# A graph network in one kernel: an extra stage in layer 2, other softmax batches, and wide products for two matrix powers

## The chip, the cores and the metric

The kernel runs on one core of a Trainium2 chip. A core has a matrix engine (TensorE, "PE" in the profile), a vector engine (VectorE, "DVE"), a scalar engine (ScalarE, "ACT"), GpSimd ("POOL") and SyncE ("SP"). Each engine works through its own queue in order, and engines wait for each other by semaphores. SP, ACT and POOL also issue DMA transfers. The metric is the device time of one execution in microseconds (us), less is better.

## What is computed

There are 50,000 nodes with 64 features and 25,000 edges sorted by destination. Four layers follow each other, each in the form x = x + layer(relu(layernorm(x))). The change touches the last two.

```python
# layer 2: attention over the edges that end in a node, 4 heads of 16
logits = sum(q[dst] * (k[src] + e_k), -1) * scale + es + clip(log(eg), -10, 10)
attn = softmax of logits over the edges of one dst
agg = segment_sum((v[src] + e_v) * attn, dst) @ Wo + bo        # then scaled and shifted by a task vector
x = layer_norm(h + agg) * g1 + b1
x = layer_norm(x + gelu(x @ W1 + b1) @ W2 + b2) * g2 + b2n

# layer 3: out = expm(-t A) h as a Taylor series, A v = segment_sum(w * v[dst], src)
for 4 substeps:
    for k in 1..20: term = scale * A(term) / k; acc += term
```

Layer 3 is a polynomial in A with known coefficients POLY[k]. Power 1 is A h, power 2 is A(A h), and so on. Only nodes with outgoing edges have a nonzero power, and higher powers reach ever fewer rows.

## The kernel before

The nodes are worked on in NQ = 49 blocks of 1024 (a tile of 128 partitions x 8 x 64). Each block has up to 640 edge slots, 5 tiles of 128. Rows of other nodes are fetched by indirect DMAs that POOL issues (helper `gather`, line 1013), 128 rows each. Sums over edges are products with one-hot matrices in bf16 on PE (`slot_hot`, lines 1945 to 1952, makes the one-hot tile `soh` on DVE). The other factor is an f32 value split into three bf16 parts (`split`, line 1089), so each sum takes three products.

**Two ways of summing.** `to_nodes` (lines 1983 to 1993) loads a 128x128 piece of `soh` as weights and streams 64 columns of values: 45 small products per block, and the result has nodes on partitions. `to_sums` (lines 1964 to 1981) loads 64 columns of values as weights and streams up to 512 columns of `soh`, with blocks 0 to 3 in the upper half of the output's partitions and blocks 4 to 7 in the lower half: 18 products per block, and the result `pa` has features on partitions, 4 groups of 128 nodes along the free axis. Layers 0 and 2 use `to_sums`.

**How stages are run.** `Steps` (line 82) and `pipeline` (line 110) run a list of stages over the blocks. In each step every block in flight does its next stage, the oldest block first, and then a new block begins. After each stage a hook is called. In layer 2 the hook is `lists_pace`, which at a rate of 0.7 per call (1.5 at the end) does one more unit of building the lists that the higher powers need: small DVE and PE instructions, and scatters and gathers on POOL's queue. In power 1 it is `rest`, at 0.34 per call, for what is left of that and for a small dense product chain (`dense`, line 2512). The framework then places the instructions into the queues, with the order of the program as priority, and sets buffers and waits: a tile with `bufs=2` makes the third use wait until the first is read.

**Layer 2** (lines 2285 to 2510) has two such pipelines. `up` has the stages fetch (5 gathers of kvg; loads of qt, keys and typ on SP's queue), hots (one-hot tiles noh and types) and logits (products pv and pe, then lg on DVE at lines 2340 to 2342). Four batches of blocks follow, 13, 12, 12 and 12. When the logits of a batch are done, `softmax` (line 2345) turns them, scans along 640 columns on DVE and turns them back into `att`. `down` works on the batch before, beside the logits of the next. Its twelve stages are fetch2, message, sums (`to_sums` and the eviction of `pa`, line 2406), attend (products with wo into `po`, then z on DVE, line 2414), spread1 (the row variance v), turn (scales z into y on DVE, line 2435, turns y by four PE transposes, line 2438, and evicts them as tr on ACT, line 2440), hidden (products ph with w1m, GELU as hid on ACT), product, spread2, finish (turns back, line 2474; x3 on DVE), spread3 and close (stores h3tab). `sums` and `turn` share one PSUM bank, `pa`; `attend` and `finish` share `po`. At line 2502:

```python
for k, (q0, n) in enumerate(batches):
    while up.done < q0 + n:
        up.step()
        if k:
            down.step(q0)
    softmax(k)
```

So the first batch has only `up` steps (the opening), the next three have an `up` and a `down` step each (mixed), and after the last softmax only `down` steps are left (the end).

**Power 1** (lines 2604 to 2632): fetch gathers 5 x 128 rows of h3tab and loads xs and h; scaled makes `soh` and the weighted, split values; sums does `to_nodes` into the PSUM tile `po`, evicts it as `f` on ACT (line 2624), stores `f` to ftab[0] from ACT's queue and adds it to xs with the coefficient. **Power 2** (lines 2638 to 2671) does the same with 2 gathers of ftab[0] per block, 39 small products (line 2663), `f` (line 2666), the store to ftab[1], and the store of xs to the output. `f` has two buffers. The gathers of a power need the whole table of the power before. **Powers 3 to 8** work on lists, with gathers and adding scatters on POOL (line 2720).

Of the kernel before, what the change touches and what calls it, by code (L numbers as in the profile page):

```python
# [22 lines left out]
F32 = mybir.dt.float32  # L23
F16 = mybir.dt.float16
# [949 lines left out]
def fast(ctx: ExitStack, tc: tile.TileContext, a: dict, out: bass.AP, flag: bass.AP):  # L974
# [956 lines left out]

    def load_keys(pool, q, s):

        s.keys = pool.tile([P, RW], F16, name="keys", bufs=4)
        nc.sync.dma_start(s.keys, ktab[q:q + 1, :].to_broadcast([P, RW]))

    def node_hot(pool, s):
# [296 lines left out]
    with tc.tile_pool(name="l1", bufs=2) as pool, \  # L2234
# [25 lines left out]
        def turn(q, s):  # L2260
            s.tr = turned(pool, ps, s.h2, "pt")
# [23 lines left out]
    with tc.tile_pool(name="l2", bufs=2) as pool, \  # L2285
# [3 lines left out]
        etab, typei, wo, bo, b1m, w1m, gcen, w2m, zb, g2c, b2n, half = (  # L2289
            getattr(cp2, x) for x in "etab typei wo bo b1m w1m gcen w2m zb g2c b2n half".split())  # L2290

        batches = [(0, 13), (13, 12), (25, 12), (37, 12)]
        batch_of = {q: k for k, (q0, n) in enumerate(batches) for q in range(q0, q0 + n)}
        S = {q: State() for q in range(NQ)}
        lgs, atts = {}, {}
# [17 lines left out]
        def logits(q, s):  # L2313
            k = batch_of[q]
            q0, n = batches[k]
            if q == q0:
                lgs[k] = pool.tile([P, 5, 13 * NH], F32, name="lg")
            vv = pool.tile([P, 5, D], F32, name="vv")
            lg = lgs[k][:, :, (q - q0) * NH:(q - q0 + 1) * NH]
            es = pool.tile([P, 5, NH], F32, name="es")  # L2320
            kk = pool.tile([P, 5, D], F32, name="kk")
            for i0, m in ((0, 3), (3, 2)):
                pv = ps.tile([P, 3, KW], F32, name="pv", bufs=2)
                for i in range(m):
                    nc.tensor.matmul(pv[:, i, :], s.types[:, (i0 + i) * P:(i0 + i + 1) * P], etab[:, :KW],
                                     start=True, stop=True)
                nc.vector.tensor_add(kk[:, i0:i0 + m, :], s.kv[:, i0:i0 + m, 0:D], pv[:, :m, 0:D])
                nc.vector.tensor_add(vv[:, i0:i0 + m, :], s.kv[:, i0:i0 + m, D:2 * D], pv[:, :m, D:2 * D])
                nc.vector.tensor_copy(es[:, i0:i0 + m, :], pv[:, :m, 2 * D:KW])  # L2329
# [12 lines left out]
            nc.vector.scalar_tensor_tensor(lg, lg, HD ** -0.5, es, op0=OP.mult, op1=OP.add)  # L2342


        def softmax(k):
            q0, n = batches[k]
            R = n * NH
            rep = pool.tile([NQ, 13, NH], F32, name="rep", bufs=1)
            nc.vector.tensor_copy(rep[:, :n, :], ident[:NQ, q0:q0 + n, None].to_broadcast([NQ, n, NH]))
            sm = pool.tile([13 * NH, RW + 1], F32, name="sm", bufs=1)  # L2350
            pen = pool.tile([13 * NH, RW + 1], F32, name="pen", bufs=1)
            rr = rep[:, :n, :].rearrange("q n h -> q (n h)")
            for c0, c1 in ((0, 512), (512, RW + 1)):
                pr = ps.tile([13 * NH, 512], F32, name="pv", bufs=2)
# [3 lines left out]
            row = pool.tile([13 * NH, RW], F32, name="row", bufs=1)  # L2358
            for i0, m in ((0, 4), (4, 1)):
                pt = ps.tile([13 * NH, 4, P], F32, name="pv", bufs=2)  # L2360
# [3 lines left out]
            f = pool.tile([13 * NH, RW], F32, name="fw", bufs=1)  # L2364
            b = pool.tile([13 * NH, RW], F32, name="bw", bufs=1)
# [9 lines left out]
            pt = ps.tile([P, 5, 13 * NH], F32, name="pe")  # L2375
            for i in range(5):
                nc.tensor.transpose(pt[:, i, :R], row[:R, i * P:(i + 1) * P], ident[:R, :R])
            atts[k] = pool.tile([P, 5, 13 * NH], F32, name="att")
            nc.scalar.activation(atts[k][:, :, :R], pt[:, :, :R], AF.Copy)


# [48 lines left out]
        def spread1(q, s):  # L2430
            spread(s, "v1")

        def turn(q, s):
            y = pool.tile([P, 8, D], F32, name="y", bufs=1)
            nc.vector.tensor_mul(y, s.z.rearrange("p i h d -> p (i h) d"), over(invert(s, "r1"), 8))
            pt = ps.tile([P, 4, P], F32, name="pa")
            for i in range(4):
                nc.tensor.transpose(pt[:, i, :], y[:, 2 * i:2 * i + 2, :].rearrange("p a d -> p (a d)"), ident)
            s.tr = pool.tile([P, 512], F32, name="tr")
            nc.scalar.activation(s.tr, pt.rearrange("p i n -> p (i n)"), AF.Copy)  # L2440

# [51 lines left out]
        def close(q, s):  # L2493
# [3 lines left out]

        lists_pace.rate, lists_pace.gap = 0.7, 5
        up = Steps(range(NQ), S, (fetch, hots, logits), lists_pace)
        down = Steps(range(NQ), S, (fetch2, message, sums, attend, spread1, turn, hidden, product, spread2, finish, spread3,  # L2500
                                      close), lists_pace)
        for k, (q0, n) in enumerate(batches):
            while up.done < q0 + n:
# [90 lines left out]
    with tc.tile_pool(name="mps", bufs=1, space=PSUM) as mps, tc.tile_pool(name="l3", bufs=2) as pool, tc.tile_pool(name="pl3", bufs=2, space=PSUM) as ps:  # L2594
# [18 lines left out]
        def scaled(q, s):  # L2613
# [3 lines left out]
                nc.scalar.activation(y3[:, i, 0, :], s.y[:, i, :], AF.Copy, scale=swgt[:, 5 * q + i:5 * q + i + 1])  # L2617
            s.parts = split(y3)

        def sums(q, s):  # L2620
            po = ps.tile([P, 8, D], F32, name="po")
            to_nodes(po, s.soh, s.parts)
            f = pool.tile([P, 8, D], F32, name="f")
            nc.scalar.activation(f, po, AF.Copy)
            nc.scalar.dma_start(nodes(ftab[0], q), f)
            nc.vector.tensor_add(s.xs, s.xs, s.h)
            nc.vector.scalar_tensor_tensor(s.xs, f, float(POLY[1]), s.xs, op0=OP.mult, op1=OP.add)
            if q < NQ - NKEPT:
                nc.sync.dma_start(nodes(xstab, q), s.xs)

        rest = Pace(itertools.chain(lists_pace.work, dense(mp, mps)), 0.34)
        pipeline(range(NQ), (fetch, scaled, sums), rest)
        rest.rest()

        l2 = lists[2]
# [18 lines left out]
            s.parts = split(y3)  # L2654

        def sums2(q, s):
            po = ps.tile([P, 8, D], F32, name="po")
            for j in range(8):
                n = 2 if j >= SECOND else 1
                for o in range(n):  # L2660
                    c = j * P + o * (OW - SECOND * P)
                    for k in range(3):
                        nc.tensor.matmul(po[:, j, :], s.soh[:, c:c + P], s.parts[:, o, k, :],  # L2663
                                         start=(o == 0 and k == 0), stop=(o == n - 1 and k == 2))
            f = pool.tile([P, 8, D], F32, name="f")
            nc.scalar.activation(f, po, AF.Copy)  # L2666
            nc.scalar.dma_start(nodes(ftab[1], q), f)
            nc.vector.scalar_tensor_tensor(s.xs, f, float(POLY[2]), s.xs, op0=OP.mult, op1=OP.add)  # L2668
            store_x(s.xs, q)

        pipeline(range(NQ), (fetch2, scaled2, sums2))


    sums = {}
# [112 lines left out]
```

## Time and profile before

| | us |
|---|---|
| median of 3 runs (lowest, highest) | 3567.95 (3559.2, 3574.22) |
| the profiled execution, whole | 3569.77 |
| its span, first to last instruction | 3568.0 |
| layer 2 in the span | 1730 to 2766 |
| power 1 in the span | 2766 to 3126 |
| power 2 in the span | 3126 to 3280 |
| powers 3 to 8 in the span | 3280 to 3568 |

How to read it: the page gives each engine's busy time and, in 40 slices of 89 us, its busy share in tenths and the clock that was granted to TensorE (5 is half speed). A row of busy times by stretch has the stretch, its length, the busy time and instruction count of PE, weight loads, DVE, ACT and POOL, the granted clock, the busy share of the DMA engines and their GB/s. A row of a wait names who waited and for whom, then the total, the number of times and the longest. A row of a group has the line, engine, operation, tiles, shape and count, then busy time and the mean in ns of one, and then the idle time just before these instructions and what ended it ("issue": nothing that the profile shows). A busy PE isn't a PE at its peak, since matmuls are pipelined. Idle time of an engine that isn't the limit costs nothing.

### The profile page before, as it was taken

What the parts mean: (1) busy time and instruction counts of PE and PEld (TensorE: products, weight loads), DVE (VectorE), ACT (ScalarE), POOL (GpSimd) and SP (SyncE); (2) the same over time, 40 slices, a digit from 0 to 9 for tenths busy, and PEclk for the clock granted to TensorE, in tenths of its full rate; (3) what the DMA queues carried; (4) which work ended last, traced back from release to release, by engine and by line L of the source; (5) the groups of instructions that cost most, each with busy time, mean ns of one, the idle gap of its engine ahead of it and who ended that gap; (6) DMA issues with size and microseconds to landing.
All of it is one profiled execution on the core that took longest, in us unless ns stands there. A gap on an engine that the chain in (4) does not pass through costs nothing. (4 is left out here: it accounts for less than half of the span.)

```text
span 3568.0 us, 62333 instructions
## 1 busy us (share of the span) xinstructions
PE 2492.4 (70%) x21184; PEld 1729.4 (48%) x21184; DVE 2620.7 (73%) x8434; ACT 1328.5 (37%) x2962; POOL 2070.2 (58%) x1955
## 2 busy tenths in 40 slices
PE   7898675399987673477669779889888554356620
PEld 3324565266665452355446445555554443356520
DVE  9999998699998882488677877777878576456410
ACT  0002553144442262377204326646667333333000
POOL 0377777655550477665374127665430787775786
PEclk9755555699996575688657667777779775567555
DMA  1003783487771362478654234343233646377221
GB/s 54 6 4 90 205 234 123 110 224 212 211 200 44 90 197 75 130 234 243 188 145 124 62 90 132 111 122 110 80 94 101 211 139 193 96 216 213 45 26 12
DMA packets 530638, 463.35 MB, mean 130 GB/s; under 512 B 281171, under 2 KB 387954, under 8 KB 530180
## 3 DMA queue, kind: packets, MB, share of 16 engines
q1 hardware_dynamic: 365012, 269.33, 26.5%
q10 hardware_dynamic: 93408, 139.47, 11.3%
q0 software_dynamic: 71888, 50.46, 7.6%
q8 instruction: 169, 2.77, 0.3%
q14 instruction: 161, 1.32, 0.1%
HBM read 226.23 MB, written 233.89 MB: 129 GB/s over the span
## 5 line engine op out<-in xcount | busy, mean ns | idle before, releaser
L1013 POOL DMA_INDIRECT kvg<-kvtab,nrs x245 | 260.6, 1064 | 307.6 <-DVE es L2329 184.0
L1013 POOL DMA_INDIRECT gt<-g1tab,nrs x245 | 243.6, 994 | 238.6 <-DVE lhot L1791 110.6
L1013 POOL DMA_INDIRECT y<-h3tab,sptr x245 | 276.8, 1130 | 138.9 <-issue 68.0
L1013 POOL DMA_INDIRECT ga<-atab,nrs x245 | 250.3, 1022 | 170.4 <-DVE z L2190 60.5
L1991 PEld LDWEIGHTS <-soh 128*128 128x128 bf16 x4410 | 221.7, 117 | 237.0 <-issue 221.8
L1013 POOL DMA_INDIRECT raw<-otab,nrd x196 | 193.4, 987 | 191.9 <-DVE bad L1159 132.5
L1981 PE MATMUL pa<-soh,m 128*64 128x256 bf16 (+3 forms) x1764 | 238.9, 348 | 25.2 <-DVE m L1093 11.6
L1018 POOL DMA_INDIRECT stab<-raw,pf x196 | 207.3, 1058 | 59.8 <-issue 59.8
L1013 POOL DMA_INDIRECT lgot<-nmap,ldst x183 | 190.1, 1039 | 75.3 <-issue 52.8
L1991 PE MATMUL po<-g,soh 128*128 128x64 bf16 x2205 | 123.3, 215 | 145.5 <-DVE g L1093 143.0
L1950 DVE TENSOR_SCALAR soh<-it,key 128x512 bf16<-128x512 f16 (+2 forms) x735 | 210.7, 332 | 1.8 <-PE pa L1981 1.6
L1991 PE MATMUL po<-y,soh 128*128 128x64 bf16 x2205 | 122.3, 228 | 125.9 <-DVE y L1093 65.4
L2272 PE MATMUL pp<-wkv,tr 64*128 64x256 f32 x784 | 151.2, 496 | 52.4 <-ACT tr L2001 52.1
L1013 POOL DMA_INDIRECT y<-ftab,ldst x140 | 138.9, 992 | 75.0 <-issue 45.7
L1093 DVE TENSOR_TENSOR y<-y 128x320 f32<-128x320 f32 (+1 forms) x196 | 75.6, 389 | 140.6 <-ACT y L2617 116.3
L1942 DVE TENSOR_SCALAR noh<-keys,pblk 128x256 bf16<-128x256 f16 (+1 forms) x784 | 176.0, 286 | 2.8 <-DMA keys<-ktab 2.7
L1196 PE MATMUL pab<-wab,tr 64*128 64x128 f32 x784 | 150.3, 437 | 32.5 <-ACT tr L1183 32.5
L1981 PEld LDWEIGHTS <-m 128*64 128x64 bf16 x1764 | 118.0, 119 | 97.9 <-issue 32.5
L1196 PEld LDWEIGHTS pab<-wab,tr 64*128 64x128 f32 x784 | 136.3, 324 | 51.5 <-ACT tr L1183 51.5
L2338 PE MATMUL pe<-qt,noh 128*128 128x64 bf16 x2205 | 157.7, 231 | 0.3 <-DVE noh L1942 0.2
L2720 POOL DMA_INDIRECT out<-y,lnode x85 | 132.4, 1558 | 38.3 <-issue 24.4
L2617 ACT ACTIVATE y<-y,swgt 128x64 f32<-128x64 f32 x245 | 82.2, 345 | 176.6 <-DMA y<-h3tab,sptr 161.1
(607 smaller groups left out, 7496.8 us busy)
## 6 DMA issues: line engine op xcount, KB each, us to landing
kvtab<-kv SPq DMA_DIRECT2D x49, 512.0 KB
ftab<-f ACTq DMA_DIRECT2D x98, 256.0 KB
xt<-in_x SPq DMA_DIRECT2D x96, 256.0 KB
btab<-bt ACTq DMA_DIRECT2D x49, 384.0 KB
bt<-btab SPq DMA_DIRECT2D x49, 384.0 KB
qtab<-qt ACTq DMA_DIRECT2D x49, 384.0 KB
qt<-qtab SPq DMA_DIRECT2D x49, 384.0 KB
xs<-xstab SPq DMA_DIRECT2D x70, 256.0 KB
```

The source lines that it names most:

```text
L1013: return nc.gpsimd.indirect_dma_start(out=dst, out_offset=None, in_=tab[:, :], in_offset=IndirectOffsetOnAxis(ap=idx, axis=0))
L1018: return nc.gpsimd.indirect_dma_start(out=tab[:, :], out_offset=IndirectOffsetOnAxis(ap=idx, axis=0), in_=src, in_offset=None, bounds_chec ...
L1093: nc.vector.tensor_sub(x3[:, :, k, :], x3[:, :, k - 1, :], h[:, :, k - 1, :])
L1196: nc.tensor.matmul(pab[:, i, :], s.tr[r, i, :], wab[r, :], start=True, stop=True)
L1942: nc.vector.tensor_scalar(s.noh[:, j, :n * P], s.keys[:, t0 * P:(t0 + n) * P], pblk[:, j:j + 1], None, op0=OP.is_equal)
L1950: nc.vector.tensor_scalar(oh[:, OHW[i]:OHW[i + 1]], it16[:, b0 * P:(b0 + n) * P], keys[:, q, i:i + 1], None, op0=OP.is_equal)
L1981: nc.tensor.matmul(o, l, r, start=(k == 0), stop=(k == len(t) - 1))
L1991: nc.tensor.matmul(po[:, j, :], oh[:, c:c + P], msg[:, i, k, :], start=(not started and i == t0 and k == 0), stop=(end and (not started or ...
L2272: nc.tensor.matmul(pp[:, i, :], s.tr[r, 2 * k + i, :], wkv[r, :], start=True, stop=True)
L2338: nc.tensor.matmul(pe[:, i, :], s.noh[:, j, c:c + P], s.qt[:, j, k, :], start=False, stop=(j == b0 + nb - 1 and k == 2))
L2617: nc.scalar.activation(y3[:, i, 0, :], s.y[:, i, :], AF.Copy, scale=swgt[:, 5 * q + i:5 * q + i + 1])
L2720: st = nc.gpsimd.indirect_dma_start(out=out[:, :], out_offset=IndirectOffsetOnAxis(ap=s.node[:, t:t + 1], axis=0), in_=sums[k][:, t, :], i ...
```

## The change

1. In layer 2, y = z x 1/std leaves `turn` and becomes a stage `scale1` of its own, ahead of it. `down` has thirteen stages. y gets two buffers instead of one, and the tile keys (used in layers 0 and 2) three instead of four.
2. The batches are 10, 13, 13 and 13 blocks. The widest is still 13, so the softmax tiles keep their shapes.
3. Powers 1 and 2 use wide products: `to_sums` in power 1, and the like of it written out in power 2 (12 products). The result `pa` is evicted as `sums` on ACT, and a fourth stage turns it by four PE transposes into `po`, which is evicted as `f` as before.

```diff
-        s.keys = pool.tile([P, RW], F16, name="keys", bufs=4)
+        s.keys = pool.tile([P, RW], F16, name="keys", bufs=3)
...
-        batches = [(0, 13), (13, 12), (25, 12), (37, 12)]
+        batches = [(0, 10), (10, 13), (23, 13), (36, 13)]
...
+        def scale1(q, s):
+            s.y = pool.tile([P, 8, D], F32, name="y")
+            nc.vector.tensor_mul(s.y, s.z.rearrange("p i h d -> p (i h) d"), over(invert(s, "r1"), 8))
+
         def turn(q, s):
-            y = pool.tile([P, 8, D], F32, name="y", bufs=1)
-            nc.vector.tensor_mul(y, s.z.rearrange("p i h d -> p (i h) d"), over(invert(s, "r1"), 8))
             pt = ps.tile([P, 4, P], F32, name="pa")
             for i in range(4):
-                nc.tensor.transpose(pt[:, i, :], y[:, 2 * i:2 * i + 2, :].rearrange("p a d -> p (a d)"), ident)
+                nc.tensor.transpose(pt[:, i, :], s.y[:, 2 * i:2 * i + 2, :].rearrange("p a d -> p (a d)"), ident)
...
+        def evict(s, pa):
+            s.sums = pool.tile([P, 4, P], F32, name="sums")
+            nc.scalar.activation(s.sums.rearrange("p i n -> p (i n)"), pa, AF.Copy)
+
+        def by_node(s):
+
+            po = ps.tile([P, 4, 2, D], F32, name="po")
+            for i in range(4):
+                nc.tensor.transpose(po[:, i].rearrange("p h d -> p (h d)"), s.sums[:, i, :], ident)
+            f = pool.tile([P, 8, D], F32, name="f")
+            nc.scalar.activation(f.rearrange("p (h i) d -> p i h d", h=2), po, AF.Copy)
+            return f
+
         def sums(q, s):
-            po = ps.tile([P, 8, D], F32, name="po")
-            to_nodes(po, s.soh, s.parts)
-            f = pool.tile([P, 8, D], F32, name="f")
-            nc.scalar.activation(f, po, AF.Copy)
+            pa = ps.tile([P, 512], F32, name="pa")
+            to_sums(pa, s.soh, s.parts)
+            evict(s, pa)
+
+        def store(q, s):
+            f = by_node(s)
             nc.scalar.dma_start(nodes(ftab[0], q), f)
...
-        pipeline(range(NQ), (fetch, scaled, sums), rest)
+        pipeline(range(NQ), (fetch, scaled, sums, store), rest)
...
         def sums2(q, s):
-            po = ps.tile([P, 8, D], F32, name="po")
-            for j in range(8):
-                n = 2 if j >= SECOND else 1
-                for o in range(n):
-                    c = j * P + o * (OW - SECOND * P)
+            pa = ps.tile([P, 512], F32, name="pa")
+            todo = ([], [])
+            for h in range(2):
+                for o, b in ((0, 4 * h), (1, max(SECOND, 4 * h))):
+                    c = b * P + o * (OW - SECOND * P)
+                    n = (4 * h + 4 - b) * P
                     for k in range(3):
-                        nc.tensor.matmul(po[:, j, :], s.soh[:, c:c + P], s.parts[:, o, k, :],
-                                         start=(o == 0 and k == 0), stop=(o == n - 1 and k == 2))
-            f = pool.tile([P, 8, D], F32, name="f")
-            nc.scalar.activation(f, po, AF.Copy)
+                        todo[h].append((pa[h * D:(h + 1) * D, (b - 4 * h) * P:512], s.parts[:, o, k, :],
+                                        s.soh[:, c:c + n]))
+            for k in range(6):
+                for t in todo:
+                    nc.tensor.matmul(*t[k], start=(k == 0), stop=(k == 5))
+            evict(s, pa)
+
+        def store2(q, s):
+            f = by_node(s)
             nc.scalar.dma_start(nodes(ftab[1], q), f)
...
-        pipeline(range(NQ), (fetch2, scaled2, sums2))
+        pipeline(range(NQ), (fetch2, scaled2, sums2, store2))
```

The additions to xs, the loads and the stores that follow each `f` are in `store` and `store2` unchanged.

More of the change, by code (lines that the diff above doesn't have):

```diff
@@ L2290, in fast @@
             getattr(cp2, x) for x in "etab typei wo bo b1m w1m gcen w2m zb g2c b2n half".split())
-        batches = [(0, 13), (13, 12), (25, 12), (37, 12)]
+        batches = [(0, 10), (10, 13), (23, 13), (36, 13)]
+        NB = max(n for _, n in batches)
         batch_of = {q: k for k, (q0, n) in enumerate(batches) for q in range(q0, q0 + n)}
@@ L2316, in logits @@
             if q == q0:
-                lgs[k] = pool.tile([P, 5, 13 * NH], F32, name="lg")
+                lgs[k] = pool.tile([P, 5, NB * NH], F32, name="lg")
             vv = pool.tile([P, 5, D], F32, name="vv")
@@ L2347, in softmax @@
             R = n * NH
-            rep = pool.tile([NQ, 13, NH], F32, name="rep", bufs=1)
+            rep = pool.tile([NQ, NB, NH], F32, name="rep", bufs=1)
             nc.vector.tensor_copy(rep[:, :n, :], ident[:NQ, q0:q0 + n, None].to_broadcast([NQ, n, NH]))
-            sm = pool.tile([13 * NH, RW + 1], F32, name="sm", bufs=1)
-            pen = pool.tile([13 * NH, RW + 1], F32, name="pen", bufs=1)
+            sm = pool.tile([NB * NH, RW + 1], F32, name="sm", bufs=1)
+            pen = pool.tile([NB * NH, RW + 1], F32, name="pen", bufs=1)
             rr = rep[:, :n, :].rearrange("q n h -> q (n h)")
             for c0, c1 in ((0, 512), (512, RW + 1)):
-                pr = ps.tile([13 * NH, 512], F32, name="pv", bufs=2)
+                pr = ps.tile([NB * NH, 512], F32, name="pv", bufs=2)
                 nc.tensor.matmul(pr[:R, :c1 - c0], rr, same[:, c0:c1], start=True, stop=True)
@@ L2357, in softmax @@
             nc.vector.tensor_scalar(pen[:R], sm[:R], -1.0, BIG, op0=OP.add, op1=OP.mult)
-            row = pool.tile([13 * NH, RW], F32, name="row", bufs=1)
+            row = pool.tile([NB * NH, RW], F32, name="row", bufs=1)
             for i0, m in ((0, 4), (4, 1)):
-                pt = ps.tile([13 * NH, 4, P], F32, name="pv", bufs=2)
+                pt = ps.tile([NB * NH, 4, P], F32, name="pv", bufs=2)
                 for i in range(m):
@@ L2363, in softmax @@
                 nc.scalar.activation(row[:R, i0 * P:(i0 + m) * P], pt[:R, :m, :], AF.Copy)
-            f = pool.tile([13 * NH, RW], F32, name="fw", bufs=1)
-            b = pool.tile([13 * NH, RW], F32, name="bw", bufs=1)
+            f = pool.tile([NB * NH, RW], F32, name="fw", bufs=1)
+            b = pool.tile([NB * NH, RW], F32, name="bw", bufs=1)
             nc.vector.tensor_tensor_scan(f[:R], pen[:R, 0:RW], row[:R], -BIG, op0=OP.add, op1=OP.max)
@@ L2374, in softmax @@
             nc.vector.tensor_mul(row[:R], row[:R], b[:R])
-            pt = ps.tile([P, 5, 13 * NH], F32, name="pe")
+            pt = ps.tile([P, 5, NB * NH], F32, name="pe")
             for i in range(5):
                 nc.tensor.transpose(pt[:, i, :R], row[:R, i * P:(i + 1) * P], ident[:R, :R])
-            atts[k] = pool.tile([P, 5, 13 * NH], F32, name="att")
+            atts[k] = pool.tile([P, 5, NB * NH], F32, name="att")
             nc.scalar.activation(atts[k][:, :, :R], pt[:, :, :R], AF.Copy)
@@ L2499, in fast @@
         up = Steps(range(NQ), S, (fetch, hots, logits), lists_pace)
-        down = Steps(range(NQ), S, (fetch2, message, sums, attend, spread1, turn, hidden, product, spread2, finish, spread3,
+        down = Steps(range(NQ), S, (fetch2, message, sums, attend, spread1, scale1, turn, hidden, product, spread2, finish, spread3,
                                       close), lists_pace)
```

## The prediction

> **What bounds the kernel now.** I read the page first, then the busy times by stretch, then the waits of layer 2 and the groups of the two power stretches, and last the timeline.
>
> ```profile
> span 3568.0 us, 62333 instructions
> ...
> PE 2492.4 (70%) x21184; PEld 1729.4 (48%) x21184; DVE 2620.7 (73%) x8434; ACT 1328.5 (37%) x2962; POOL 2070.2 (58%) x1955
> ...
> PEclk9755555699996575688657667777779775567555
> ```
>
> No engine is full over the span, so each stage has a limit of its own. The stretches below are layer 2 (opening, first mixed part, rest of the mixed part, end), power 1 and power 2.
>
> ```profile
> core 0: us, PE busy (x) PEld busy (x) DVE busy (x) ACT busy (x) POOL busy (x), PEclk, DMA share, GB/s
> 1730.00:1852.00 122.00, 73.31 (x842) 54.28 (x841) 82.88 (x341) 6.11 (x12) 86.86 (x82) 0.50 0.58 168
> 1852.00:2125.00 273.00, 222.15 (x1696) 140.15 (x1697) 214.07 (x894) 89.38 (x131) 80.34 (x74) 0.68 0.33 96
> 2125.00:2545.00 420.00, 372.71 (x2467) 229.26 (x2463) 328.12 (x1094) 246.68 (x349) 271.50 (x256) 0.74 0.38 113
> 2545.00:2766.00 221.00, 187.05 (x950) 111.45 (x949) 178.72 (x553) 151.27 (x242) 48.03 (x45) 0.84 0.31 96
> 2766.00:3126.00 360.00, 177.15 (x2365) 151.49 (x2366) 217.06 (x539) 118.21 (x334) 276.82 (x245) 0.63 0.53 159
> 3126.00:3280.00 154.00, 93.63 (x1919) 87.97 (x1918) 92.25 (x244) 57.92 (x147) 99.17 (x98) 0.71 0.87 244
> ```
>
> In the opening POOL sets the pace: the timeline has a kvg gather every 1.25 to 1.4 us, five to a block, and the logits of two blocks 6.7 us apart (lg at 1826.7 and 1833.5). In the mixed part and the end PE is busy 81 to 89% and DVE 78 to 81%; both lose time to each other:
>
> ```profile
> POOL kvg L1013 <- DVE es L2329: 184.0, 15, 33.4
> ACT tr L2440 <- PE pa L2438: 107.0, 35, 6.8
> ...
> DVE z L2414 <- PE po L2412: 88.0, 27, 6.9
> ...
> PE ph L2448 <- ACT hid L2450: 16.5, 20, 2.1
> ...
> PE pa L2438 <- DVE y L2435: 10.3, 9, 2.7
> ```
>
> POOL waits there for buffers that DVE frees, so it isn't the limit. In the powers it is:
>
> ```profile
> L1013 POOL DMA_INDIRECT y<-h3tab,sptr x243 | 274.9, 1131 | 74.1 <-issue 67.7 <-ACT y L2617 3.0 <-DMA y<-h3tab,sptr 2.7
> L1013 POOL DMA_INDIRECT y<-ftab,ldst x98 | 99.2, 1012 | 43.5 <-issue 33.5 <-ACT y L2653 6.7 <-DMA y<-ftab,ldst 2.4
> L2663 PE MATMUL po<-y,soh 128*128 128x64 bf16 x1911 | 92.5, 221 | 57.3 <-ACT f L2666 33.8 <-DVE y L1093 14.8 <-ACT y L2653 6.6
> ...
> L1981 PE MATMUL pa<-soh,m 128*64 128x256 bf16 (+3 forms) x1764 | 238.9, 348 | 25.2 <-DVE m L1093 11.6
> ```
>
> In power 1 (2770 to 3126 here) gathers and their gaps make 274.9 + 74.1 = 349 of 356 us. In power 2 (to 3277) they make 142.7 of 151, and the DMA engines are 87% busy.
>
> **The scaled rows.** No instruction is added: r1 (0.18 us) and y (0.68 us) are issued one step earlier, ahead of the next turn instead of in it. DVE's order inside a step stays (finish, y, reduce, z). PE's transposes of y no longer wait for DVE in the same step: 10.3 us of PE waits go. Behind them ACT waits 107 us for tr, and PE waits 16.5 us for hid, which queues on ACT behind tr; I credit a fifth of that, 3 us. What is late next is z behind the attend products (88 us), PE's own pace, so nothing more is credited. Bounds: -27 (both PE waits go whole) and, since every queue's order can change with a stage more, a loss that rival D prices at 39. Taken: -13, near the row that goes for certain. The second y buffer is paid with one of four keys buffers: in layer 2 typ, with two buffers on the same SP queue, stands behind it and is tighter; in layer 0 keys still come two steps before their use. DVE's wait for keys is 2.7 us in the whole kernel (the page's group of L1942), so 0, and +3 if it doubles. The thirteenth stage makes the drain one step longer, but the same instructions; PE works until 2755 of 2766, so I put 1 us on the last latency.
>
> **The batches.** The opening covers 10 blocks instead of 13: 3 x 6.7 = -20.1 us, of POOL's pace. The three blocks move into mixed steps (39 instead of 36). There each costs PE, from the group rows between 2080 and 2310, 29.6/9.0 + 10.3/9.2 + 8.6/11 = 5.2 us, three 15.6; PE idles 51 of 273 us in the first mixed part, to which they go. Cost between 0 and 15.6; taken 8. The hooks that feed the list building come later with the three blocks: nine hooks x 0.7, six units, +3 (a unit costs DVE and PE a few tenths of a us each: from 0.3-us rows such as lhot's). The end has 13 starts instead of 12, but the pipe behind them is no fuller: 247 stage calls of 13 (19.0 blocks) for 222 of 12 (18.5), which the mixed part is rid of: 0. Softmax instructions run over 640 columns whatever the rows: 0. Sum -9, bounds -20 and -1 (+6 if a unit costs three times that).
>
> **The powers.** Per block 45 (power 1) or 39 (power 2) narrow products become 18 or 12 wide ones, an ACT eviction (0.59 us, 7.1/12 in the rows of L2406) and four f32 transposes. PE before: 92.5/49 = 1.9 us in power 2, 2.5 in power 1. After: the wide products of layers 0 and 2 take 238.9/98 = 2.4 us a block (the halves overlap: 18 x 0.348 would be 6.3), a burst at clock 0.95 took 1.49, the transposes 0.66 at full clock and 1.12 at half. Power 2 has as many columns in its longer half (3 x 1024). So 2.15 us at full clock, some 2.1/c at clock c. In power 1 a block has 7.2 us of POOL: hidden, and POOL's own waits are 6 us: 0. In power 2 a block has 154/49 = 3.1 us: at 0.71, 49 x 2.96 = 145 us and 21 us of waits for y make 166, +12; on the other side, products that no longer wait for f (33.8 us of PE waits) let the stage run closer to POOL, up to -9 (its 6.7 + 2.4 us of waits). Taken: -2, because f's two buffers and their stores (20 us of ACT's waits) stay as they are. ACT goes from 58 to 87 of 154 us. Both stages end with a chain that nothing covers: +0.59 and +1.1 less a shorter burst, +1.5 each. Sum +1, bounds -9 and +64 (next part).
>
> The trace grants 0.71 in power 2 and 0.99 to 1.00 where PE hardly pauses. The Trainium skill (TensorE: Matmul & The Clock Gate, Part 1) says that the clock is halved by default and released by some 3.4 us of steady work: by it a busier PE in power 2 would earn the full clock, 105 us and no cost; by the row 145. Against the change stands TensorEngine Tiling, Key Properties: a change of tiling mode drains TensorE, and each block now changes twice; in layer 2 the wide products followed transposes at 2444.6 without a gap, so I add nothing.
>
> **Sum.** -13 + 1 - 9 + 1 = -20. The profiled execution took 3569.8 us (span 3568.0 and 1.8 around it), 1.8 over the median of 3567.95: 3548.
>
> **Rivals.**
> - A, the forecast, 3548 (3536 to 3560): 0.44.
> - B, the waits change places: z behind PE takes the 13 us, the three blocks cost their full 15.6 + 3. Then 0 + 1 - 1.5 + 1, nothing: 3568. For it: PE is 89% busy from 2125 on. 0.18.
> - E, the queues loosen more: if earlier transposes halve DVE's 88 us for z and that ends last, -44 instead of -13: 3517. For it: a step without list work took 14.0 us (z at 2443.3 and 2457.3) where the mean of 36 is 693/36 = 19.3. Against: most of the rest is list work. 0.16.
> - C, slower: PE becomes the bound of power 2. Its place is the wide products with transposes, its price 49 x 3.95 us (1.49 x 0.95/0.5 + 1.12 at half clock) + 21 = 215 for 154, +61: 3609. It decides from a clock of about 0.77 down (2.1/c + 0.4 over 3.1 us). For it: 0.71 now. Against: more work, fewer pauses. 0.10.
> - D, slower: a new order of instructions in layer 2's queues costs 1 us in each of 39 mixed steps and the y wait returns elsewhere: 3548 + 39 = 3587. For it: steps differ by 5 us already. 0.12.
>
> **Chances.** About 0.5% is what a measurement of this kernel can tell from no change, 3550 and 3586 here. Faster: E and 0.28 of A, 0.44. Within: the other 0.16 of A and 0.14 of B, 0.30. Slower: C, D and the rest of B, 0.26. The range goes from half way beyond E, 3512, to beyond D, 3598.
>
> **What would show it.** Right: no row of PE waiting for y in layer 2; first lg of the second batch some 20 us earlier in the stage; layer 2 some 20 us shorter; power 1 still 349 us of gathers; power 2 within 10 us of 154. Wrong: a longer wait of z or of the first products in place of y's; POOL idle in power 2 with a clock near 0.5; layer 0 longer than 515 us (keys).

## The result and the profile after

The changed kernel takes 3593.61 us (median of 20 runs, 3566.15 to 3617.29). The kernel before, run beside it on the same chip, takes 3568.95 (20 runs, 3559.2 to 3579.44). The ratio is 1.0064, 95% interval 1.0044 to 1.0084: slower by 23 us, 16 to 30. The forecast was 3548, faster by 20. The time lies inside the predicted range, but on the other side of "before".

When e13 to e16 ran, every kernel, the kernel before beside them included, took some 1120 us longer, so of these four only the ratios to that kernel before are used.

The profiled execution after took 3590.18 us, span 3588.4. From its page, the span, the busy times and the granted clock:

```profile
span 3588.4 us, 57871 instructions
...
PE 2580.9 (72%) x18930; PEld 1686.0 (47%) x18930; DVE 2627.9 (73%) x8434; ACT 1353.9 (38%) x3046; POOL 2046.7 (57%) x1955
...
PEclk9755555699996575788567658667788786688555
```

The powers' narrow products are gone (PE has 2254 instructions less), ACT has 84 more, and the clock is higher in the slices of the powers (34 to 37: 6, 6, 8 and 8 tenths, before 5, 5, 6 and 7). Where the time went shows only by stretch. These are layer 2 (opening, mixed part, end), power 1 and power 2 of the kernel after, cut at the eviction of the first and the last `att`, and at the first gather of each power:

```profile
core 0: us, PE busy (x) PEld busy (x) DVE busy (x) ACT busy (x) POOL busy (x), PEclk, DMA share, GB/s
1731.00:1831.00 100.00, 58.47 (x660) 42.81 (x661) 70.39 (x277) 5.96 (x12) 70.47 (x67) 0.50 0.61 172
1831.00:2563.00 732.00, 618.59 (x4327) 380.18 (x4326) 551.65 (x2060) 310.64 (x459) 359.51 (x345) 0.72 0.36 104
2563.00:2801.00 238.00, 198.85 (x963) 117.21 (x961) 182.63 (x547) 157.59 (x248) 47.05 (x45) 0.80 0.31 94
2801.00:3156.00 355.00, 227.80 (x1238) 131.06 (x1238) 218.71 (x537) 140.09 (x383) 267.91 (x246) 0.73 0.55 161
3156.00:3300.00 144.00, 111.77 (x792) 60.78 (x792) 95.33 (x241) 80.71 (x196) 97.58 (x98) 0.94 0.93 257
```

The same cuts in the kernel before are at 1740.4 (first kvg), 1852.1, 2545.7, 2767.5, 3128.7 and 3338.5 (first row of the powers 3 to 8). The lengths, cut alike:

| us | before | after | difference |
|---|---|---|---|
| opening, from the first kvg gather | 111.7 | 91.0 | -20.7 |
| mixed part (36 and 39 steps) | 693.6 | 731.3 | +37.7 |
| end | 221.8 | 238.3 | +16.5 |
| power 1 | 361.2 | 354.9 | -6.3 |
| power 2, to the first row of the list powers | 209.8 | 203.3 | -6.5 |

So layer 2 lost 34 us (opening, mixed part, end) and the powers won 13. The waits of layer 2 after (who waited for whom, total, times, longest), the rows that answer to those of before and the new ones:

```profile
...
ACT L2453 <- PE ph L2451: 104.5, 28, 12.5
DVE z L2415 <- PE po L2413: 81.6, 24, 14.2
ACT v L2472 <- PE pv L2470: 80.2, 18, 25.6
...
ACT tr L2443 <- PE pa L2441: 42.9, 15, 8.6
...
PE pa L1981 <- DVE m L2394: 9.0, 7, 3.8
...
PE ph L2451 <- ACT zt L2463: 7.0, 9, 1.6
...
PE pa L2441 <- DVE y L2436: 4.4, 3, 2.8
```

What the change aimed at happened: PE's wait for y fell from 10.3 to 4.4 us and ACT's for tr from 107.0 to 42.9. In their place ACT waits 104.5 us for the hidden products (24.3 before) and 80.2 for the products pv of spread2 (21.0 before), and PE waits for m and zt, where it hardly did.

### The profile page after: what moved, and what is told of

It reads as the page before. It is cut to its first block, busy times and chain, and to the rows that moved or that the text cites. A ratio compares the mean times of both kernels' runs of the same rounds, so it can differ in the third digit from the quotient of the medians.

```text
span 3588.4 us, 57871 instructions
## 1 busy us (share of the span) xinstructions
PE 2580.9 (72%) x18930; PEld 1686.0 (47%) x18930; DVE 2627.9 (73%) x8434; ACT 1353.9 (38%) x3046; POOL 2046.7 (57%) x1955
## 5 line engine op out<-in xcount | busy, mean ns | idle before, releaser
L1013 POOL DMA_INDIRECT y<-h3tab,sptr x245 | 267.8, 1093 | 171.6 <-DVE soh L1950 97.2
L1981 PE MATMUL pa<-soh,m 128*64 128x512 bf16 (+3 forms) x1764 | 258.3, 364 | 37.1 <-DVE m L1093 15.3
L1981 PE MATMUL pa<-soh,y 128*64 128x256 bf16 (+3 forms) x882 | 138.1, 412 | 87.3 <-DVE soh L1950 61.7
L2451 PE MATMUL ph<-tr,w1m 64*128 64x256 f32 x392 | 144.4, 496 | 24.6 <-ACT hid L2453 16.2
L1991 PEld LDWEIGHTS <-soh 128*128 128x128 bf16 x2205 | 107.9, 114 | 97.9 <-issue 94.6
L1139 ACT ACTIVATE ln_v<-ln_v,epsc 128x8 f32<-128x8 f32 x147 | 43.9, 298 | 276.6 <-DVE ln_v L1138 258.8
L2339 PE MATMUL pe<-qt,noh 128*128 128x64 bf16 x2205 | 141.5, 221 | 0.2
```

What stands on the lines that cost most here:

```text
L1013: return nc.gpsimd.indirect_dma_start(out=dst, out_offset=None, in_=tab[:, :], in_offset=IndirectOffsetOnAxis(ap=idx, axis=0))
L1139: nc.scalar.activation(v, v, AF.Sqrt, bias=epsc, scale=1.0 / D)
L1981: nc.tensor.matmul(o, l, r, start=(k == 0), stop=(k == len(t) - 1))
L1991: nc.tensor.matmul(po[:, j, :], oh[:, c:c + P], msg[:, i, k, :], start=(not started and i == t0 and k == 0), stop=(end and (not started or ...
L2451: nc.tensor.matmul(ph[h][:, c:c + 256], w1m[r, :], s.tr[r, c:c + 256], start=True, stop=True)
```

## The experiments

First theory: the moved y makes every round of layer 2 dearer, because the queues get a new order (rival D's mechanism). Second theory: it is only the depth of the pipeline, and the batches do the rest. In brackets after a ratio stands its 95% interval. The us behind it are that ratio times the median of the kernel before, run beside it, less that median, with the interval's ends.

**The parts alone.** Each is the kernel before with one part of the change's diff. e1 has the scale stage, y's second buffer and three keys buffers. e2 has the batches, e3 the powers. e4 has a stage that does nothing in the new one's place:

```diff
+        def idle(q, s):
+            pass
...
-        down = Steps(range(NQ), S, (fetch2, message, sums, attend, spread1, turn, hidden, ...
+        down = Steps(range(NQ), S, (fetch2, message, sums, attend, spread1, idle, turn, hidden, ...
```

> The kernel before with the scaled rows in a stage of their own and three keys buffers; batches and powers as before. The whole change lost 34 us in layer 2 and won 13 in the powers, so something in layer 2 is dearer. Theory 1 (the move of y itself makes every step of the lower pipeline dearer, as rival D had it: the end part took 237 us for 221, and a mixed step kept its 19 us though it has less list work): +20 to +30 us. Theory 2 (a stage more only costs one more step in which the pipe runs out, 8 us by the last stores of h3tab, which leave every 3.5 to 9 us; the rest of the loss is the batches'): +5 to +10 us. My prediction had -12.

> The kernel before with the batches 10, 13, 13, 13 alone. The opening gets 20.7 us shorter in either theory (att of the first batch came that much earlier in the whole change). Theory 1: the three blocks cost some 27 us in the mixed steps (9.15 us an upper block beside lower work), net +7. Theory 2: they cost more, because in the second batch three of its steps start no lower block (10 blocks are ready for 13 steps), so that the lower pipe has a hole: net +17 to +25. My prediction had -9.

> The kernel before with the wide products and transposes in powers 1 and 2 alone. In the whole change power 1 took 355 us for 361 and power 2 took 141 for 148. Both theories: -13 us, layer 2 unchanged. Rival: part of that gain is an accident of where the stages stood after layer 2, then 0 to -5. My prediction had +1.

> The kernel before with a stage in the place of the new one that does nothing, so that the lower pipeline has thirteen stages and the hook of the list building is called once more per block; y is still made in the turn stage. Theory 1 (it is the move of y): -3 to +4 us. Theory 2 (it is the depth): the same +5 to +10 as with y moved.

Measured: e1 1.0047 [1.0032, 1.0063], +17 (11 to 23). e2 1.0019 [1.0, 1.0037], +7 (0 to 13). e3 0.9957 [0.9939, 0.9975], -15 (-22 to -9). e4 1.0011 [0.9995, 1.0027], +4 (-2 to 10). So the powers win, the batches lose a little, as the first theory had it (+7), and y in a stage of its own loses most. The empty stage's +4 is not clear of zero. Neither theory had e1 right: 17 lies below the first one's 20 and above the second one's 10. In e4 and e1 the end takes 229.3 and 232.3 us for 221.8, which speaks for depth, and in these two profiles the mixed part is as long as before (693.5 and 695.4). So of e1's 17 us some 10 lie in the end by its profile, and next to none in the mixed steps. (Some 8 us of e1's profile lie ahead of layer 2, as 7 of e4's do: the starts of layer 2 in these profiles lie between 1738 and 1749, in code that no experiment touches but for keys.)

**Depth and y apart.** e5 takes a stage away from the kernel before, e8 does the same beside the moved y, so that it has twelve stages again. e7 has both layer 2 edits without the powers.

```diff
             s.parts = split(m3)
+            lists_pace()
+            if q + 1 < NQ:
+                fetch2(q + 1, S[q + 1])
...
-        down = Steps(range(NQ), S, (fetch2, message, sums, ...
+        down = Steps(range(NQ), S, (message, sums, ...
```

> The kernel before with one lower stage less: the loads of fetch2 for the next block are issued at the end of message, in the place in the order where they stood, so that the lower pipeline has eleven stages (the hook is still called twelve times per block); y stays in turn. Theory 2 (depth: each lower stage is one more step at the end, 7.5 us in the profile of the empty stage, 10.5 in that of the scale stage, 221.8 us of end before): -7 to -10 us, all of it in the end part (212 to 215 us). Rival: the longer ends of the two were chance between executions, or came from the hook called more often: 0 (-3 to +3).

> Both layer 2 edits without the powers. The single edits gave +17 and +7 by the times, and the powers -13; together the change gave +23, so 14 us more than the sum. If the two edits really add to each other (the mixed part of the whole change took 731 us for 720 with the batches and 695 with the scale stage alone): +34 to +40. If the sum is the truth and the rest is uncertainty of the intervals (6 us each way): +20 to +28.

> The kernel before with y in a stage of its own (three keys buffers) and fetch2 issued from message, so that the lower pipeline has twelve stages as before. Theory 1 (the move of y itself costs, 13 us by the difference of the scale stage, +17, and the empty one, +4): +8 to +13. Theory 2 (only the depth cost): within 4 us of the kernel before, the end part within 4 us of 222. My prediction's reason (PE no longer waits for y in the same step): -13.

Measured: e5 0.9994 [0.9978, 1.001], -2 (-8 to 4), end 222.3. e8 1.0078 [1.0053, 1.0102], +28 (19 to 36). e7 1.0067 [1.0047, 1.0088], +24 (17 to 31). The second theory, that it is only the depth, falls: a stage less at the front brings nothing, and with the old depth the moved y costs as much as the whole loss, and more than the first theory's 13. In e8 the mixed part takes 725.3 us (690.1 in e5) and the end 220.1: here the loss is in the mixed steps. e7 is the sum of e1 and e2 (17 + 7) by the times.

**The batches the other way.** e6 has batches of 24 and 25, with one buffer each for lg and att.

> The kernel before with two batches, 24 and 25 (lg and att with one buffer each, for room); everything else as before. With the batches 10, 13, 13, 13 the opening got 22.5 us shorter (7.5 a block) and the mixed part 26 longer (8.7 a block). Theory 2a (a block's logits cost more beside lower work, where PE is 86% busy, than in the opening, where POOL sets the pace; lower work costs the same anywhere): 11 blocks moved the other way bring 11 x 1.2 = 13, and two softmaxes go, some 5 to 10 us each: -15 to -33 us. Theory 2b (what cost the time was the hole in the lower pipe, 10 blocks for 13 steps; beside a full pipe the logits are nearly free): opening +82, mixed part shorter by the lower work alone, and the end without logits beside it longer by as much: +30 to +60 us.

Measured: 1.0017 [1.0001, 1.0033], +6 (0 to 12). Both theories miss. The opening took 71 us more, the mixed part 226 less, the end 159 more. How the blocks are divided hardly matters over this span. In e2 the row of the mixed part shows why three blocks more in it cost as much as the opening wins:

```profile
1830.00:2549.00 719.00, 615.85 (x4336) 382.97 (x4336) 553.85 (x2048) 329.02 (x474) 361.19 (x345) 0.71 0.37 107
```

PE is busy 616 us where the kernel before has 595 in its 694, so 21 us more, 7 a block. PE's idle time is 103 us, 99 before. None of the three blocks' work shows up there.

**The order of the queues.** The same products stand in another order on PE when y is ready a step sooner. I take it that the framework puts an instruction ahead when it expects its operands earlier; that is argued from the order and not shown. The timeline of PE shows one round without list work of the kernel before (start, duration, operation; in brackets the idle time before it and what ended it):

```profile
2356.39 0.49 PE L2412 MATMUL po<-wo,sums 128*128 128x128 f32 x2
2356.71 0.60 PE L2438 MATMUL pa<-ident,y 128*128 128x128 f32 x4
...
2358.43 1.86 PE L1981 MATMUL pa<-soh,m 128*64 128x512 bf16 x16
...
2362.47 1.05 PE L2467 MATMUL pv<-half,sqt 128*128 128x2 f32 x8 [0.54 <-DVE es L2329]
...
2365.11 0.34 PE L2325 MATMUL pv<-etab,types 24*128 24x132 bf16 x3
...
2369.09 2.05 PE L2454 MATMUL ph<-tr,gcen 128*128 128x512 f32 x2
```

and the same of e1:

```profile
2369.11 0.60 PE L2440 MATMUL pa<-ident,y 128*128 128x128 f32 x4
...
2373.72 1.39 PE L2469 MATMUL pv<-half,sqt 128*128 128x2 f32 x8 [2.02 <-DVE es L2329]
2374.97 2.05 PE L2456 MATMUL ph<-tr,gcen 128*128 128x512 f32 x2
2376.96 0.51 PE L2325 MATMUL pv<-etab,types 24*128 24x132 bf16 x3
...
2382.41 2.61 PE L1981 MATMUL pa<-soh,m 128*64 128x512 bf16 x7
...
2385.27 1.16 PE L2412 MATMUL po<-wo,sums 128*128 128x128 f32 x8
2386.36 0.74 PE L1981 MATMUL pa<-soh,m 128*64 128x256 bf16 x9
```

Before, the order is attend with the transposes of y, to_sums, pv, logits, gcen. In e1 w1m no longer stands between the transposes of zt and pv, which now waits 2.02 us for DVE's es; gcen stands ahead of the logits, and to_sums is cut in two by attend. Over layer 2, e1's PE waits 10.7 us for m (0.5 before), 11.1 for zt (2.6) and 10.0 for the v of spread2 (1.5). Its waits for y are 9 us less and those for x of finish 10 less. All its waits together are 153 us, 124 before. That sum isn't the cost, though: in e10, which is 22 us faster than e1, PE's waits come to 155 us. The same 630 products of to_sums in the mixed part tell more. In the kernel before, in e1, in e10 and in e17 (the last two hold the old order, see below) their rows are:

```profile
L1981 PE MATMUL pa<-soh,m 128*64 128x512 bf16 (+3 forms) x630 | 76.0, 362 | 5.2 <-ACT tr L2440 4.4 <-DVE m L2393 0.5
L1981 PE MATMUL pa<-soh,m 128*64 128x512 bf16 (+3 forms) x630 | 92.2, 397 | 12.9 <-DVE m L2393 8.7 <-DVE m L1093 2.0 <-ACT tr L2442 1.6
L1981 PE MATMUL pa<-soh,m 128*64 128x256 bf16 (+3 forms) x630 | 65.5, 333 | 14.4 <-ACT tr L2455 13.6 <-DVE m L2395 0.5
L1981 PE MATMUL pa<-soh,m 128*64 128x512 bf16 (+3 forms) x630 | 75.3, 362 | 4.2 <-ACT tr L2444 4.2
```

With y moved and the order free they take 16 us more of PE's time, with y moved and the order held 11 less. The trace's clock records say why: 165 of the 630 ran for the most part at half clock before (154 in e9 and 212 in e3, whose layer 2 has the order of before), 284 in e1, 70 in e10 and 168 in e17. Other products gained in e1 (gcen took 933 ns for 1070), and its mixed part as a whole is no longer than before.

e9 has three keys buffers and nothing else. In e10 y stays moved, and the old order is put back by hand; e11 and e12 do so for both layer 2 edits and for the whole change.

```diff
 def sums(q, s):
-            to_sums(pa, s.soh, s.parts)
+            with tc.issue_after(last["attend"]) if "attend" in last else ExitStack():
+                to_sums(pa, s.soh, s.parts)
...
 def product(q, s):
-            nc.tensor.matmul(pz, gcen, s.tr, start=True, stop=False)
+            with tc.issue_after(last["logits"]):
+                nc.tensor.matmul(pz, gcen, s.tr, start=True, stop=False)
...
 def attend(q, s):
+            if "turn" in last:
+                with tc.issue_after(last["attend"]):
+                    turned1(*last.pop("turn"))
```

(`issue_after` queues what is inside it behind the given instruction. `last` holds the last attend and logits product, and the block whose turn is due; `turned1` is turn's body. The lines that fill `last` are left out.)

> The kernel before with three keys buffers instead of four and nothing else (the queues keep the order of before). Theory 1 (what costs is the new order of the queues that comes with the moved y): 0, within 4 us. Rival K (the loads of keys come too late in layers 0 and 2; the scale kernels all had three buffers and cost 17 to 30 us): +10 to +20, layer 0 longer and DVE waiting for keys in layer 2.

> The kernel of e1 (y in a stage of its own, thirteen stages, three keys buffers) with PE's old order of work in layer 2: the transposes of turn follow the attend products of the same step, to_sums follows them, and the product with gcen follows the logits. In the kernel before the most frequent round on PE is attend, turn, w2m, to_sums, zt, w1m, pv, w1m, logits, gcen, w2m; with y moved the transposes of turn are ready early, and the rounds became attend, turn, w1m, turn, zt, gcen, pv, to_sums, logits, w2m, w1m and the like, with new waits of PE (to_sums for DVE's m 0.5 to 10.7 us, ph for ACT's hid and zt 23 to 45). Theory 1 (the order is what costs): within 6 us of the kernel before, where e1 had +17, and those waits back near before's. Rival (the stage itself costs, by y's second buffer or the longer way of a block through the pipe): +11 to +20 as in e1.

> Both layer 2 edits (e7, +24 to +28) with PE's old order held as in e10. Theory 1: the moved y costs nothing, and the batches alone remain: +3 to +12. Rival: +20 to +30 as in e7.

> The whole changed kernel with PE's old order in layer 2 held as in e10. Theory 1: the batches' +7 and the powers' -15: -12 to -2 against the kernel before, where the change has +23. Rival: +15 to +25.

Measured: e9 0.999 [0.9972, 1.0007], -4 (-10 to 3). e10 0.9986 [0.997, 1.0001], -5 (-11 to 0). e11 1.0018 [1.0002, 1.0034], +6 (1 to 12). e12 1.0002 [0.9988, 1.0016], +1 (-4 to 6). Keys cost nothing that can be told from noise. Holding the old order wins 22 us in e10 against e1, 18 in e11 against e7 and 22 in e12 against the change. In e12's profile the mixed part takes 709.4 us and the end 232.2, where the change has 731.3 and 238.3. That the order of PE's queue is worth some 20 us here is thus shown three times. That it is the moved y that spoiled the order doesn't follow from that, as e17 shows below. e12 itself missed what was expected (-12 to -2) by a little. The mixed part and the end of e10:

```profile
1847.00:2526.00 679.00, 554.83 (x4135) 350.80 (x4135) 535.52 (x1983) 314.74 (x459) 338.88 (x330) 0.75 0.37 107
2526.00:2758.00 232.00, 191.29 (x975) 116.10 (x976) 185.22 (x561) 160.22 (x251) 47.50 (x46) 0.82 0.32 97
```

The mixed part is 15 us shorter than before, the end 10 longer. e10's PE waits 0.5 us for m and 1.0 for zt, as in the kernel before; its 10.4 for v of spread2 stayed as in e1.

**What of it is y, and what the order.** e13 holds only to_sums, e14 only gcen. e15 and e17 are one kernel, the kernel before with both held and y still in turn. e16 and e18 are one kernel, e10 with the wide powers.

> The kernel of e1 (y moved, thirteen stages) with one thing held: to_sums follows the attend products of its step; gcen, w1m and the transposes of turn stand where the framework puts them. If it is to_sums that came too early (PE waits for DVE's m: 0.5 us before, 10.7 in e1) and delayed attend, and with it z: -5 to +6 against before. If not: +12 to +20, as e1.

> The kernel of e1 with the other thing held: the product with gcen follows the logits. If it is gcen ahead of the logits that costs (it takes the second ph buffer early, and PE waits for hid and zt on ACT, 23 us before, 45 in e1): -5 to +6 against before. If not: +12 to +20. If each place costs a part: +5 to +12 in both runs.

> The kernel before, y still in turn, twelve stages, with to_sums held behind attend and gcen behind the logits. If the gain of e10 (mixed part 679 us for 694, end 232 for 222, whole -5) comes from the moved y: 0, mixed part 690 to 698. If it comes from holding the order in the steps where list work had moved it: -5 to -15, mixed part near 680.

> The kernel of e10 with the wide powers, old batches: the change without its batches, with PE's old order held. If the parts add: -5 and -15, so -14 to -24 against the kernel before, below both kernels (and near the time that I forecast for the change, 3548). If the powers' gain fades as in e12 (-3 for the expected -8): -5 to -12.

> The kernel of e15 again (the kernel before, y still in turn, to_sums held behind attend and gcen behind the logits), in the usual condition. If the moved y brings what e10 won: 0, mixed part 690 to 698 us. If the held order brings it: -5 to -15, mixed part near 680, end near 222.

> The kernel of e16 again (y moved, order held, wide powers, old batches), in the usual condition: -14 to -24 against the kernel before if the parts add, 3543 to 3553; -5 to -12 if the powers' gain fades beside it.

Measured: e13 1.0023 [1.0003, 1.0043], e14 1.0058 [1.0045, 1.0071], e15 0.9964 [0.9953, 0.9976], e16 0.9931 [0.9918, 0.9945]. Run again, e17 0.9955 [0.9939, 0.997], -16 (-22 to -11), and e18 0.9958 [0.9941, 0.9975], -15 (-21 to -9). Holding gcen alone leaves the loss, holding to_sums alone seems to take part of it (1.0023 against e1's 1.0047, intervals that overlap, and not run beside each other). Neither alone reaches e10. e16 and e18 are one kernel and hardly agree, so these four ratios can't be set beside the others closely. The surprise is e17: the order held, with y where it was, beats e10. Its two rows:

```profile
1856.00:2540.00 684.00, 581.11 (x4163) 365.87 (x4163) 543.53 (x1992) 335.67 (x480) 351.43 (x330) 0.73 0.37 108
2540.00:2761.00 221.00, 185.26 (x949) 110.08 (x948) 177.85 (x551) 150.41 (x240) 47.86 (x45) 0.83 0.32 97
```

So of the 15 us that e10 wins in the mixed part, 10 come from the held order and at most 5 from the moved y, and its stage gives 10 back in the end. The four kernels side by side, against the kernel before:

| us | order free | order held |
|---|---|---|
| y in turn | 0 | -16 (e17) |
| y in a stage of its own | +17 (e1) | -5 (e10) |

Holding the order wins 22 us with the moved y and 16 without it, and the moved y costs 17 us with the order free and 11 with it held. The difference of 6 is within the noise (each entry is known to some 6 us, and e10 and e17 were not run beside each other). By the times the two seem to act each for itself, and that the moved y is slow because of its new order is not shown. The profiles say more, with one execution each. In the mixed part the moved y adds 2 us (e1), 35 (e8 over e5) and 11 to 12 (e7 and the change over e2) with the order free, and takes 4 to 5 off with it held. In the end the thirteenth stage adds its 7 to 10 us with the order free (e4, e1) and held (e10, e12).

e17, e18 and e3 beat both kernels, by 15 or 16 us against the kernel before. e17's order with e3's powers and y in turn was not tried, and neither was the held order with the new batches and y in turn.

## Why the prediction was wrong, by its own steps

- **The scaled rows, "-13", are where it failed.** The step said that DVE's order stays and "what is late next is z behind the attend products", "so nothing more is credited". The first half held, z's wait even fell (88.0 to 81.6), and PE's wait for y went as forecast (1.3 us in e1 for 10.3). But what the wait had cost did not come off the time. In place of -13 the whole edit measured +17 (e1), and +28 at the old depth (e8). I had stated that "every queue's order can change with a stage more" and used it as a bound only, although to_sums, gcen and w1m did leave their places in PE's queue. Even with the order held, y is worth 5 us of the mixed part, not 13.
- **The extra stage's drain, "+1", was too small.** The argument was "the same instructions". The end grew by 7.5 (e4) to 10.5 us (e1). Why a stage less at the front brought nothing (e5, 222.3) stays open. In e1's profile this term is more than half of the edit's loss; what the rest of it is, and how much of e8's 32 us in the mixed part the new order explains, stays open too, since e8 was not run with its order held.
- **Rival D had named the new order**, and its 3587 is nearest to the measured 3594. That is in part luck: its 1 us in each of 39 mixed steps came out as 0.05 (e1) to 0.9 (e8) and 0.3 in the change over e2, and the end and the batches, which it took as forecast, made up the rest.
- **The batches, "-9".** The opening was right: -20.1 forecast, -20.7 and -22.5 (e2) measured. The end was near: 0, and +2 in e2, though "13 starts instead of 12" was a slip: both kernels have 13, the kernel before because its 36 mixed steps start 36 blocks of 49, the changed one because three of its 39 steps have no block to start. The failed term is the three blocks in mixed steps, "+8" with "+3" for hooks: 26 us in e2. I priced a block at 5.2 us of PE and let half of it vanish in PE's idle time; it took 7, and none vanished. All batches: +7, not -9.
- **The powers, "+1", in the right bounds on the wrong side.** Measured -15 (e3). Power 1 fell by 6 to 8 us, where I had put 0: its gathers took 1086 to 1093 ns for 1130. But other kernels with the narrow products had power 1 between 353 and 364 us, so that only some 6 us are the change's, between the means of 12 and 4 profiles (358.8 and 352.6). Power 2 fell by 6, near the bound of "up to -9". Its stretch and group rows in e3:

```profile
3124.00:3268.00 144.00, 114.54 (x792) 62.30 (x792) 95.24 (x241) 80.75 (x196) 100.27 (x98) 0.92 0.91 255
L1013 POOL DMA_INDIRECT y<-ftab,ldst x98 | 100.3, 1023 | 41.7 <-issue 31.7 <-ACT y L2668 4.0 <-DMA y<-ftab,ldst 3.3
L2683 PE MATMUL pa<-soh,y 128*64 128x512 bf16 x441 | 84.1, 413 | 12.9 <-ACT y L2668 7.6 <-DVE y L1093 4.5 <-DVE soh L2663 0.7
```

  POOL's 100.3 + 41.7 = 142 us still fill the stretch of 144, as 142.7 did 151. PE's wait of 33.8 us for f is gone. But the gain did not come by POOL's waits, from which the bound was taken: they were 9.1 us and are 7.3. What else shortened the stretch is not shown. The work was priced well: PE's 114.5 us in 49 blocks at a clock of 0.92 are 2.15 us a block at full clock, the figure of the prediction. (The burst of 1.49 us in it ran at 1.00 by the trace, not at 0.95; that makes C's price 7 us higher and changes nothing else.)
- **Rival C is refuted.** The busier PE got 0.92 (e3) and 0.94 (after) where the narrow products had 0.71. The +12 at the row's 0.71, one side of this step, did not come either. The Trainium skill (TensorE: Matmul & The Clock Gate, Part 1) has the clock released by steady work; here the measurement agrees with it, and C's half clock did not come.
- **Keys, "0"**, was right (e9).
- **The sum.** e1 + e2 + e3 make 17 + 7 - 15 = +9, with some 11 either way; the change measured +23 (16 to 30). By the profiles' stretches the two layer 2 edits add to each other (+10 and +5 alone, +32 together, though e7's profiled execution is the longest of its six), by the times they do not (e7). Seen from the other side, the powers, worth 15 us alone, brought 6 beside both layer 2 edits with the order held (e12 against e11) and 1 with it free (the change against e7). That difference of 14 is not settled. The runs of the change also spread over 51 us, those of before over 20, and no experiment explains that.

The signs of the prediction that came true were the opening and power 2 within 10 us of 154; the wait for y, which was to be gone, fell to 4.4 us. Layer 2 was to get 20 us shorter and got 34 longer, and of the signs of being wrong, a longer wait of "z or of the first products" named the wrong instructions: it was above all ACT's wait for the hidden products and for pv of spread2.

## What to carry to other kernels

Taking a wait away from one instruction can reorder its engine's whole queue where a framework places the instructions; so compare the order of the queue before and after. Hold the old order beside the change, and hold it in the kernel before as well: here that alone won 16 us, and without e17 the 22 us of e10 would all have been put down to the moved y. A smaller wait is no gain by itself, and a larger sum of waits no loss (153 us in e1, 155 in e10). Where PE was 86% busy, a block that was moved into the mixed part cost its full PE time (7 us), and PE's idle time was no store to pay from. A stage more cost 7 to 10 us in the run-out with the same instructions.

## What the runs showed of the hardware

Off PE nothing ran longer by itself in the slower kernels: evictions of 128x512 by `sums` took 0.59 to 0.60 us, gathers had a median of 0.95 us, and an ACT table load took 1283 ns in all of them. On PE one product's time goes with the granted clock of its moment: in the mixed part a to_sums product of 128x512 took 385 ns on average at 1.00 and 630 at 0.50 in the kernel before, and 393 and 635 in e1, so what it costs depends on when it runs. The other unexpected part was the clock in power 2. With PE busy 62% of the stretch (93.63 of 152 us) 0.71 was granted, with 80% (114.54 of 144) 0.92. The busy share alone doesn't decide it: in layer 2's opening PE is busy 60% (67.61 of 112 us) and has 0.50.
